# A two-layer graph network on one core: edge lags kept through the heads, last output products moved to the second period, layer 1's row splits and inverse degrees moved behind its keys and values

## The chip, the core and the metric

The kernel runs on one core of a Trainium2 chip. A core has five engines that run at the same time, each with its own list of instructions: the PE (TensorE, matrix products, with a separate record PEld for its weight loads), DVE (VectorE), ACT (ScalarE), POOL (GpSimd) and SP (SyncE, which here only issues transfers). They meet at semaphores. Transfers between the large memory (HBM) and the on-chip memory (SBUF) run on 16 DMA engines; they are issued from the queues of SP, ACT and POOL, and an instruction that issues a transfer can stand in its queue until what it needs is there. Products are summed up in a small memory of their own, PSUM.

The metric is the device time of one execution in microseconds (us), the median of several runs.

## What is computed

625 nodes with 1024 features, 10,000 edges. Two layers; each adds a graph part and an attention part that read the same normalized rows, and then a feed-forward part:

```python
edge_index = jnp.stack([src, dst])
xn = _layernorm(x)
x = x + _L0_gnn_ref(xn, edge_index, ...) + _L0_mix_ref(xn[None], ...)[0]
x = x + _L0_ffn_ref(_layernorm(x)[None], ...)[0]
xn = _layernorm(x)
x = x + _L1_gnn_ref(xn, src, dst, ...) + _L1_mix_ref(xn[None], ...)[0]
x = x + _L1_ffn_ref(_layernorm(x)[None], ...)[0]
```

The parts that the change touches:

```python
# layer 0, graph: attention over edges (4 heads of 64), with a loop at each node
e = jnp.einsum('ehd,hd->eh', leaky_relu(xl[src] + xr[dst], 0.2), att)
out = segment_sum(softmax_over_dst(e)[..., None] * xl[src], dst).reshape(n, 256) @ W_up
# both layers, attention without softmax (16 heads of 64, phi = elu + 1)
kv, ksum = einsum('nd,ne->de', phi(k), v), phi(k).sum(0)
out = (phi(q) @ kv) / (phi(q) @ ksum + eps) @ W_o + b_o
# layer 0, feed-forward with three-valued weights
silu(gate(x)) * up(x) -> down
# layer 1, graph: mean over incoming edges, twice
h = relu(x @ W_self0 + (sum_in(x) / max(deg, 1)) @ W_neigh0 + b0)
out = h @ W_self1 + (sum_in(h) / max(deg, 1)) @ W_neigh1 + b1
```

Layer 1's feed-forward part (attention, then eight experts of which each row uses two, and a shared one) is not touched by the change.

## The kernel before

The 625 rows stand in five blocks of 125 (NT = 5, index t); the 1024 features in eight blocks of 128 (KC = 8, index k or m); weights of 1024 columns are loaded in halves of 512 (class Half, index c), two transfers of 1 MB for each half, through a ring of buffers (wpool). The order on each engine is written out by hand. The helper `do` (class Stream) takes a piece of PE work and the vector work that follows it, and issues the vector work of one piece behind the PE work of a later one.

**Start (lines 361 to 570).** Rows are loaded, normalized and turned; edge numbers (si, di), att, the projection weights, the biases and the attention's weights are loaded. On SP's queue stand the rows, small weights, then the filling of `table` with zeros (625 x 625 pairs of nodes, padded, by 4 heads: 6.3 MB in HBM), and then, from `lin.half(0)`, the biases bk_t and bv_t and the weights Wk and Wv of layer 0's first half. The edge numbers and att are the first on ACT's queue. `left_right` makes xl and xr, which are written to HBM (xl_d, xr_d); `self_loops` makes the scores of the nodes' own loops, which are written to the table's diagonal (table<-own).

**Edges beside layer 0's attention (lines 575 to 790).** The 79 edge columns (128 edges each, the last 16) are worked in groups of two. For each column POOL issues a gather of xl rows (ga), a gather of xr rows (gb) and a scatter of the scores into the table, all indirect DMAs. A scatter waits for the landing of the one before. DVE adds, scales and reduces a group (lines 600, 572, 573), ACT takes the exponential (line 579). The function `work(us)` advances a planned clock by the PE work just issued, and issues the next group ("beat") when the clock passes its due time: 5.2 us a group at first, 8.5 from the seventh on. `lags` says how many groups score, exponential and scatter stand behind the gathers of the same beat; the value is cut by one for the last two of the eight heads (m >= 6), and set to 1, 1, 2 after them. What is left when the PE work is all issued follows in a loop without pacing.

Meanwhile the PE makes keys and values of both halves, then for every pair of heads m the query pq (line 130 through `query`), pd and po (`answer`; DVE then adds, takes the reciprocal, line 338, and multiplies: oT, line 339), and then the output products px with Wo, by `mixed(t)`: sixteen products for each block t. The sums of t = 3 and t = 4 are moved out of PSUM by DVE with the bias added (`kept`), since PSUM holds only three blocks (t = 0, 1, 2). Behind each block's px one of the three weight matrices of the feed-forward part is made three-valued by DVE (`ternary`).

**Feed-forward of layer 0, in periods p = 0 to 6 (lines 1011 to 1075).** The table is read back in five blocks (`load_table(t)`, tile tb, on POOL's queue), multiplied with the edge counts (`weigh`, tile pT, line 821), and multiplied with xl on the PE (`sums`, pg; then go, turned to goT, and `up_again`, px on top of the output products). Period p has sums of block p, and for block p - 1 the feed-forward: normalized rows, turned (ptr), gate and up (pgu), turned (phT), down (pdn), normalized again and turned (xnT1). The rows x are loaded again on POOL's queue, between the first block of the table and the second. From period 2 keys and values of layer 1 are put between (`spacer`); their weights are loaded by `lin1.weights(0)` in period 1.

**Layer 1 (lines 1077 to 1215).** Second half's keys and values, degrees (`degrees`), heads again by `query` and `answer`, and then the products of the mean (pa). For these the normalized rows are needed as two numbers, high and low (`rows_of`, `split`: DVE line 1144, ACT line 1117, DVE line 1119), ten pieces (two halves c, five blocks t). They and the inverse degrees (`inverses`) stand between the heads: two pieces after each of m = 0 to 3, one after m = 4 and 5, then the inverses. The biases b1 and bo are added to x on POOL (line 1161) after the heads.

Of the kernel before, what the change touches and what calls it, by code (L numbers as in the profile page):

```python
# [53 lines left out]
def attempt(ctx: ExitStack, tc: tile.TileContext, w: dict, out: bass.AP, shifted: bool):  # L54
# [161 lines left out]
    class LinearAttention:  # L216
# [17 lines left out]
        def half(self, c, loaded=False):  # L234
            Wk, bk, Wv, bv = (w[n] for n in self.names[1:])
            self.bk, self.bv = self.bias(bk, c, "bk_t"), self.bias(bv, c, "bv_t")
            if not loaded:
                self.weights(c)
            self.kf = mid([P, NT, 512], "kf")
            self.v = mid([P, NT, 4, 129], "v")  # L240
            nc.gpsimd.memset(self.v[:, :, :, 128:129], 1.0)
            self.kv.append(mix.tile([128, 4, 256], FP, tag="kv", name="kv", bufs=2))
# [101 lines left out]
    with ExitStack() as st0:  # L344
# [8 lines left out]
        with ExitStack() as edges:  # L353
# [10 lines left out]
            for dst, name in ((si, "src"), (di, "dst")):  # L364
                flat = w[name].rearrange("a b -> (a b)")
                nc.scalar.dma_start(out=dst[:, 0:EF], in_=flat[0:128 * EF].rearrange("(p t) -> p t", t=EF))
                nc.scalar.dma_start(out=dst[0:ER, EF:EN], in_=flat[128 * EF:E].rearrange("(p t) -> p t", t=1))
# [5 lines left out]
            for t in range(2, NT):  # L373
# [5 lines left out]
            nc.scalar.dma_start(out=att, in_=w["att"].to_broadcast([128, 256]))  # L379
# [5 lines left out]
            nc.gpsimd.memset(none, FAR if shifted else 0.0)  # L385
            nc.sync.dma_start(out=table.rearrange("(p a b) h -> p a (b h)", p=128, a=28),
                              in_=none.unsqueeze(1).to_broadcast([128, 28, 440]))
            sf = pool.tile([128, EN], FP, name="sf")
# [5 lines left out]
            def edge_numbers():  # L394
                for dst, src in ((sf, si), (df, di)):
                    nc.vector.memset(dst[:, EF:EN], -1.0)
                    nc.vector.tensor_copy(dst[:, 0:EF], src[:, 0:EF])
                    nc.vector.tensor_copy(dst[0:ER, EF:EN], src[0:ER, EF:EN])


                nc.vector.tensor_scalar(up, df, float(HN), None, op0=ALU.is_ge)
                nc.vector.scalar_tensor_tensor(dm, up, -float(HN), df, op0=ALU.mult, op1=ALU.add)
                nc.vector.tensor_scalar(up, up, 4095.0, 1.0, op0=ALU.mult, op1=ALU.add)

                row, col = (df, sf) if shifted else (sf, df)
                nc.vector.scalar_tensor_tensor(at, row, float(N), col, op0=ALU.mult, op1=ALU.add)
# [3 lines left out]
            if not shifted:  # L410
                nc.vector.tensor_scalar(att, att, 0.8, None, op0=ALU.mult)
# [128 lines left out]
            turn_x(1)  # L540
            root(0)
            for t in range(NT):
# [9 lines left out]
                if t == NT - 2:  # L552
# [4 lines left out]
            lin = LinearAttention(xnT, ("L0_Wq", "L0_Wk", "L0_bk", "L0_Wv", "L0_bv"), w["L0_bq"],  # L557
                                  lambda us: work(us), nc.sync)
            lin.half(0)
# [121 lines left out]
            def work(us):  # L681
                beat["us"] += us

                while beat["us"] >= 2.0 + 5.2 * min(beat["g"], 6) + 8.5 * max(beat["g"] - 6, 0) and chunks:
                    one_beat()
# [32 lines left out]
            def mixed(t, ks=range(KC), keep=None, then=None):  # L718
                for c in range(2):
                    def pe(c=c):  # L720
                        if c == 0 and ks[0] == 0:
                            hold["px", t] = ps2("px1")
                        for k in ks:
                            nc.tensor.matmul(hold["px", t][:P, c, :], lhsT=oT[:, k, nodes(t)], rhs=wo[c](k),  # L724
                                             start=(k == 0), stop=(k == KC - 1 and keep is not None))

                    def after():
                        px = hold.pop(("px", t))
                        for c in range(2):
                            nc.vector.tensor_tensor(keep[:, c, :], px[:P, c, :], bo[c][:P], op=ALU.add)  # L730

                    do(None, pe, after if keep is not None and c == 1 else None)
                    if then is not None and c == 0:
                        then()
                    work(0.87 * len(ks))
# [29 lines left out]
            for m in range(KC):  # L765
                if m >= KC - 2:
                    lags[:] = [n - 1 for n in lags]
                if m + 1 < KC:
                    lin.query(m + 1)
                else:  # L770
                    mixed(0, range(6))
# [15 lines left out]
            kept = mid([P, 2, 2, 512], "kept")  # L787
            mixed(3, keep=kept[:, 0], then=weight_sums)
            mixed(4, keep=kept[:, 1])
            weight_means()  # L790
            mixed(0, range(6, KC))
# [84 lines left out]
        def up_again(t):  # L876
            kept_apart = t >= 3
# [137 lines left out]
        load_table(1)  # L1015
# [9 lines left out]
        for p in range(NT + 2):  # L1025
# [6 lines left out]
            if p == 1:  # L1032
                lin1.weights(0)
# [23 lines left out]
            for t in ((0, 1), (2, 3, 4))[p] if p < 2 else ():  # L1057
                for c in range(2):
                    xc = x[:, t, c * 512:(c + 1) * 512]
                    nc.vector.tensor_tensor(xc, xc, bo[c][:P] if t < 3 else kept[:, t - 3, c, :], op=ALU.add)  # L1060
            if p == 1:
                lin1.half(0, loaded=True)
# [45 lines left out]
    def inverses():  # L1108
        nc.vector.reciprocal(dinv, dinv)
        own = mix.tile([P, NP], FP, tag="qe", name="own", bufs=1)[:, 0:N].rearrange("p (t n) -> p t n", t=NT)  # L1110
        nc.vector.tensor_tensor(own, dinv[:P, 0:N].rearrange("p (t n) -> p t n", t=NT),
                                ident[:P, :P].unsqueeze(1).to_broadcast([P, NT, P]), op=ALU.mult)
        nc.vector.tensor_reduce(dinvT, own, AX.X, ALU.add)
# [15 lines left out]
    degrees()  # L1129
    for t in range(1, NT):  # L1130
        lin1.key(t)
        lin1.value(t)
# [4 lines left out]

    xnh = [[midp.tile([P, NT, 512], NUM, tag="mid", name="xnh") for i in range(2)]]
    xnh.append([midp.tile([P, NT, 512], NUM, tag="mid", name="xnh"), sage.tile([P, NT, 512], NUM, name="xnl")])
    rows_left = [(c, t) for c in range(2) for t in range(NT)]  # L1140

    def rows_of(c, t):
        xh = mix.tile([P, 512], FP, tag=("kb", "ke")[t % 2], name="xh", bufs=1)
        nc.vector.tensor_scalar(xh, x[:, t, c * 512:(c + 1) * 512], mv1[:, t, 0:1],
                                rs1[:, t:t + 1], op0=ALU.subtract, op1=ALU.mult)
        split(xh, xnh[c][0][:, t, :], xnh[c][1][:, t, :])

    for m in range(KC - 1):
        lin1.query(m + 1)
        lin1.answer(m, oT)  # L1150
        for _ in range(2 if m < 4 else 1):
            if rows_left:
                rows_of(*rows_left.pop(0))
        if m == 5:
            inverses()
    assert not rows_left
    for name in ("b1", "L1_bo"):
        b_t = mix.tile([128, D], FP, tag="kv", name="b_t", bufs=2)
        nc.gpsimd.dma_start(out=b_t, in_=w[name].to_broadcast([128, D]))
        for t in range(NT):  # L1160
            nc.gpsimd.tensor_tensor(x[:, t, :], x[:, t, :], b_t[:P], op=ALU.add)
# [23 lines left out]
    for m in range(KC):  # L1185
        if m % 4 == 0:
            ws, wn = Half(wpool, w["W_self0"], m // 4), Half(wpool, w["W_neigh0"], m // 4)
            hT.append(mid([128, 4, NP], "hT"))
        a = m % 4
# [745 lines left out]
```

## Time and profile before

| | |
|---|---|
| median of 3 runs | 2213.21 us (2208.89 to 2214.76) |
| profiled execution | 2212.67 us |
| its span, first to last instruction | 2210.6 us |
| mean granted clock of the PE | 0.978 of full |
| transfers | 301.62 MB, 136 GB/s on the mean |
| POOL's scatters, page's row: table<-es,at | x79, 83.9 us, 1062 ns each |
| POOL's gathers: ga<-xl_d,si and gb<-xr_d,di | x79 each, 1041 and 998 ns |

The span is the time between the first and the last instruction in the record; the rest of the time of that execution lies outside of it. A row of a group has the line, engine and operation, the tiles written and read, the count, the busy time and the mean of one in ns, and then the idle time just before these instructions with what ended it. "PE pg L130 <- DVE pT L821" in a list of waits means: the PE stood before the product pg, issued at line 130, until DVE had written pT at line 821. The record of a product with float32 operands is two records of the PE. The row PEclk is the clock that the PE was granted, in tenths; at half clock a product takes twice as long, and this time counts as busy.

### The profile page before, as it was taken

What the parts mean: (1) busy time and instruction counts of PE and PEld (TensorE: products, weight loads), DVE (VectorE), ACT (ScalarE), POOL (GpSimd) and SP (SyncE); (2) the same over time, 40 slices, a digit from 0 to 9 for tenths busy, and PEclk for the clock granted to TensorE, in tenths of its full rate; (3) what the DMA queues carried; (4) which work ended last, traced back from release to release, by engine and by line L of the source; (5) the groups of instructions that cost most, each with busy time, mean ns of one, the idle gap of its engine ahead of it and who ended that gap; (6) DMA issues with size and microseconds to landing.
All of it is one profiled execution on the core that took longest, in us unless ns stands there. A gap on an engine that the chain in (4) does not pass through costs nothing. (4 is left out here: it accounts for less than half of the span.)

```text
span 2210.6 us, 17366 instructions
## 1 busy us (share of the span) xinstructions
PE 2119.9 (96%) x6934; PEld 1215.4 (55%) x6934; DVE 714.3 (32%) x1216; ACT 194.3 (9%) x354; POOL 342.3 (15%) x351
## 2 busy tenths in 40 slices
PE   7999997869899989999999999999999999999998
PEld 5665573445455667754446767457744444444443
DVE  4786486467421760000122133322011111111012
ACT  2010110002211200000000111100000000000000
POOL 1666776400000120010000000110000000000011
PEclk9999999869999999999999999999999999999999
DMA  9335432620122110240213111122099988997742
GB/s 293 92 98 180 146 113 79 161 66 22 44 80 76 48 48 1 76 161 20 76 38 105 38 39 38 29 95 94 8 361 345 331 306 295 330 330 285 275 143 92
DMA packets 145849, 301.62 MB, mean 136 GB/s; under 512 B 12371, under 2 KB 22437, under 8 KB 145755
## 3 DMA queue, kind: packets, MB, share of 16 engines
q1 hardware_dynamic: 123412, 243.18, 31.0%
q0 software_dynamic: 17664, 47.47, 7.1%
q10 hardware_dynamic: 4678, 9.72, 1.4%
q8 instruction: 58, 0.95, 0.2%
q14 instruction: 37, 0.30, 0.0%
HBM read 277.49 MB, written 22.84 MB: 136 GB/s over the span
## 5 line engine op out<-in xcount | busy, mean ns | idle before, releaser
L130 PE MATMUL pu<-w,xgT 128*128 128x512 f32 x768 | 333.9, 593 | 1.9 <-DVE xgT L1229 1.9
L130 PEld LDWEIGHTS pu<-w,xgT 128*128 128x128 f32 x768 | 144.0, 190 | 174.8 <-issue 171.9
L130 PE MATMUL pyb<-w,hb 128*128 128x512 f32 x384 | 174.3, 598 | 2.5 <-ACT yb L105 2.1
L130 PE MATMUL pk<-w,xnT 128*125 128x512 f32 x320 | 143.9, 603 | 3.8 <-DMA w<-in_L_Wk_dram 3.2
L130 PE MATMUL pv<-w,xnT 128*125 128x512 f32 x320 | 141.2, 594 | 0.0
L130 PE MATMUL pq<-xnT,w 128*128 128x313 f32 x512 | 138.1, 428 | 2.0 <-ACT qf L320 1.2
L130 PE MATMUL p<-tT,w 128*128 128x313 f32 x512 | 136.3, 428 | 0.4 <-DVE tT L1229 0.4
L130 PEld LDWEIGHTS pyb<-w,hb 128*128 128x128 f32 x384 | 69.8, 189 | 90.9 <-issue 74.8
L130 PEld LDWEIGHTS pq<-xnT,w 128*128 128x128 f32 x512 | 96.5, 190 | 42.1 <-ACT qf L320 3.7
L1769 DVE TENSOR_TENSOR su<-pu,su 128x512 f32<-128x512 f32 x24 | 16.6, 692 | 314.6 <-ACT su L1768 314.6
L130 PEld LDWEIGHTS p<-tT,w 128*128 128x128 f32 x512 | 96.8, 190 | 37.9 <-issue 1.2
L130 PEld LDWEIGHTS pk<-w,xnT 128*125 128x125 f32 x320 | 60.3, 191 | 77.8 <-issue 76.0
L130 PEld LDWEIGHTS pv<-w,xnT 128*125 128x125 f32 x320 | 60.0, 189 | 72.4 <-issue 71.8
L610 POOL DMA_INDIRECT table<-es,at x79 | 83.9, 1062 | 63.2 <-issue 33.7
L1752 POOL DMA_INDIRECT xg<-rows_d,slots x12 | 11.4, 947 | 524.7 <-PE pxg L1759 449.0
L592 POOL DMA_INDIRECT ga<-xl_d,si x79 | 82.3, 1041 | 29.6 <-issue 19.8
L592 POOL DMA_INDIRECT gb<-xr_d,di x79 | 78.9, 998 | 24.1 <-issue 23.5
L724 PE MATMUL px<-w,oT 128*125 128x512 f32 x160 | 71.1, 605 | 11.3 <-DVE z L337 11.3
L1119 DVE TENSOR_TENSOR z<-pz,z 125x512 fp32r<-125x512 f32 x10 | 6.9, 692 | 196.8 <-ACT z L1117 196.8
L130 PE MATMUL px<-w,hT 128*125 128x512 f32 x160 | 70.3, 592 | 0.0
L130 PE MATMUL px<-w,oT 128*125 128x512 f32 x160 | 70.3, 592 | 0.0
L130 PE MATMUL ph<-meanT,w 128*128 128x313 f32 x256 | 70.0, 426 | 0.0
(368 smaller groups left out, 2538.9 us busy)
## 6 DMA issues: line engine op xcount, KB each, us to landing
w<-in_eW_dram SPq DMA_DIRECT2D x144, 1024.0 KB
w<-in_L_Wk_dram SPq DMA_DIRECT2D x8, 1024.0 KB
w<-in_L_Wv_dram SPq DMA_DIRECT2D x8, 1024.0 KB
w<-in_L_Wq_dram SPq DMA_DIRECT2D x8, 1024.0 KB
w<-in_L_Wo_dram SPq DMA_DIRECT2D x8, 1024.0 KB
w<-in_W_self_dram SPq DMA_DIRECT2D x8, 1024.0 KB
w<-in_W_neigh_dram SPq DMA_DIRECT2D x8, 1024.0 KB
w<-in_sW_dram SPq DMA_DIRECT2D x8, 1024.0 KB
```

The lines of the kernel that those rows point to most:

```text
L130: nc.tensor.matmul(dst, lhsT=lhsT, rhs=rhs, start=(i == 0), stop=(i == len(pairs) - 1))
L592: nc.gpsimd.indirect_dma_start(out=ab[g][side][0:p, j, :], out_offset=None, in_=src[:, :], in_offset=bass.IndirectOffsetOnAxis(ap=ix[0:p, ...
L610: nc.gpsimd.indirect_dma_start(out=table[:, :], out_offset=bass.IndirectOffsetOnAxis(ap=at[0:p, lo + j:lo + j + 1], axis=0), in_=es[0:p, l ...
L724: nc.tensor.matmul(hold["px", t][:P, c, :], lhsT=oT[:, k, nodes(t)], rhs=wo[c](k), start=(k == 0), stop=(k == KC - 1 and keep is not None))
L1119: nc.vector.tensor_tensor(low, src, high.bitcast(FP), op=ALU.subtract)
L1752: nc.gpsimd.indirect_dma_start(out=xg, out_offset=None, in_=rows_d[:, :], in_offset=bass.IndirectOffsetOnAxis(ap=slots[:, b:b + 1], axis=0))
L1769: nc.vector.tensor_tensor(su, pu[:, 0, :], su, op=ALU.mult)
```

## The change

- **Start.** The loads of the edge numbers and of att move on ACT's queue behind `turn_x(1)`; att's scaling moves into `edge_numbers`. Biases and Wk of layer 0's first half are issued on SP's queue ahead of the zeros of the table, Wv behind them.
- **Edges.** A group from the seventh on is due every 8.1 us instead of 8.5. Lags are no longer cut in the last two heads, and the first output products, which stand in the last head, no longer advance the plan's clock.
- **Last output products.** `mixed(4)` moves from in front of the first period into period 1 (the second one), its halves at two places; its result stays in PSUM, and the bias is added as for t < 3. Layer 1's loads of Wk and Wv come behind it.
- **Table.** The second block of the table is loaded behind the first block of x instead of behind all five.
- **Layer 1.** The inverse degrees, in two pieces, and the five row splits of the first half go behind keys and values of t = 1 to 4. The heads m = 0 to 4 keep one row split each. The additions of b1 and bo on POOL move behind the heads and the mean products, to the stage of hT (m = 0 and m = 4), and their loads go to SP's queue.

```diff
@@ start @@
-            for dst, name in ((si, "src"), (di, "dst")):
-                ...
-            nc.scalar.dma_start(out=att, in_=w["att"].to_broadcast([128, 256]))
+            def load_edges():
+                for dst, name in ((si, "src"), (di, "dst")):
+                    ...
+                nc.scalar.dma_start(out=att, in_=w["att"].to_broadcast([128, 256]))
+            lin = LinearAttention(xnT, ("L0_Wq", "L0_Wk", "L0_bk", "L0_Wv", "L0_bv"), w["L0_bq"],
+                                  lambda us: work(us), nc.sync)
+            lin.biases(0)
+            lin.wk = Half(wpool, w["L0_Wk"], 0)
             nc.sync.dma_start(out=table.rearrange("(p a b) h -> p a (b h)", p=128, a=28),
                               in_=none.unsqueeze(1).to_broadcast([128, 28, 440]))
+            lin.wv = Half(wpool, w["L0_Wv"], 0)
             turn_x(1)
+            load_edges()
             root(0)
-            lin.half(0)
+            lin.half(0, loaded=True, biased=True)
@@ edges @@
-                while beat["us"] >= 2.0 + 5.2 * min(beat["g"], 6) + 8.5 * max(beat["g"] - 6, 0) and chunks:
+                while beat["us"] >= 2.0 + 5.2 * min(beat["g"], 6) + 8.1 * max(beat["g"] - 6, 0) and chunks:
-            def mixed(t, ks=range(KC), keep=None, then=None):
-                for c in range(2):
+            def mixed(t, ks=range(KC), keep=None, then=None, paced=True, cs=(0, 1)):
+                for c in cs:
-                    work(0.87 * len(ks))
+                    if paced:
+                        work(0.87 * len(ks))
-                if m >= KC - 2:
-                    lags[:] = [n - 1 for n in lags]
-                    mixed(0, range(6))
+                    mixed(0, range(6), paced=False)
-            kept = mid([P, 2, 2, 512], "kept")
-            mixed(3, keep=kept[:, 0], then=weight_sums)
-            mixed(4, keep=kept[:, 1])
+            kept = mid([P, 2, 512], "kept")
+            mixed(3, keep=kept, then=weight_sums)
+            mixed(0, range(6, KC))
             weight_means()
-            mixed(0, range(6, KC))
@@ periods @@
-            kept_apart = t >= 3
+            kept_apart = t == 3
             rows_dma(nc.gpsimd, x[:, t, :], xrows[t])
-        load_table(1)
+            if t == 0:
+                load_table(1)
             if p == 1:
-                lin1.weights(0)
+                mixed(4, cs=(0,))
-                    nc.vector.tensor_tensor(xc, xc, bo[c][:P] if t < 3 else kept[:, t - 3, c, :], op=ALU.add)
+                    nc.vector.tensor_tensor(xc, xc, kept[:, c, :] if t == 3 else bo[c][:P], op=ALU.add)
             if p == 1:
+                mixed(4, cs=(1,))
+                lin1.weights(0)
                 lin1.half(0, loaded=True)
@@ layer 1 @@
+    meanwhile = inverses() + [lambda t=t: rows_of(0, t) for t in range(NT)]
     for t in range(1, NT):
-        lin1.key(t)
-        lin1.value(t)
+        for f in (lin1.key, lin1.value):
+            f(t)
+            if meanwhile:
+                meanwhile.pop(0)()
     for m in range(KC - 1):
         lin1.query(m + 1)
         lin1.answer(m, oT)
-        for _ in range(2 if m < 4 else 1):
-            if rows_left:
-                rows_of(*rows_left.pop(0))
-        if m == 5:
-            inverses()
-    for name in ("b1", "L1_bo"):
-        ...
+        if m < NT:
+            rows_of(1, m)
         if m % 4 == 0:
             ws, wn = Half(wpool, w["W_self0"], m // 4), Half(wpool, w["W_neigh0"], m // 4)
             hT.append(mid([128, 4, NP], "hT"))
+            b_t = mix.tile([128, D], FP, tag="kv", name="b_t", bufs=2)
+            nc.sync.dma_start(out=b_t, in_=w[("b1", "L1_bo")[m // 4]].to_broadcast([128, D]))
+            for t in range(NT):
+                nc.gpsimd.tensor_tensor(x[:, t, :], x[:, t, :], b_t[:P], op=ALU.add)
```

In `rows_of`, the pieces of the first half write their normalized rows to the buffers of qf; those of the second half use kb and ke as before. `inverses` returns its two pieces instead of issuing them.

## The prediction

> **What bounds the kernel now.** I read the busy shares first, then the waits of the PE (TensorE), then the windows by stage, then the time order of the places where the PE waits. The page says:
>
> ```profile
> span 2210.6 us, 17366 instructions
> PE 2119.9 (96%) x6934; PEld 1215.4 (55%) x6934; DVE 714.3 (32%) x1216; ACT 194.3 (9%) x354; POOL 342.3 (15%) x351
> PEclk9999999869999999999999999999999999999999
> ```
>
> The PE is busy for 2119.9 of 2210.6 us, and the change removes no matrix product. So it can win only PE idle time and time in which the PE runs at half clock, which counts as busy. The windows by stage show where both are (columns: window, length, busy time and instructions of PE, PEld, DVE, ACT, POOL, granted clock, DMA share, GB/s):
>
> ```profile
> 0.00:48.00 48.00, 34.62 (x220) 28.56 (x220) 26.62 (x82) 12.52 (x26) 7.67 (x19) 1.00 0.90 277
> 48.00:409.00 361.00, 347.87 (x1255) 209.31 (x1256) 243.23 (x446) 35.51 (x95) 244.40 (x237) 0.98 0.36 117
> 409.00:448.00 39.00, 26.88 (x74) 15.70 (x72) 6.43 (x9) 1.66 (x2) 11.28 (x19) 0.73 1.00 255
> 448.00:630.00 182.00, 158.38 (x573) 92.99 (x574) 111.27 (x225) 34.30 (x56) 6.24 (x11) 0.88 0.19 58
> 630.00:707.00 77.00, 77.00 (x230) 39.92 (x229) 12.69 (x20) 7.22 (x13) 0.00 (x0) 1.00 0.16 55
> 707.00:812.00 105.00, 93.35 (x365) 66.55 (x364) 77.13 (x62) 16.77 (x25) 26.24 (x14) 0.95 0.15 51
> 812.00:2210.00 1398.00, 1381.85 (x4225) 762.38 (x4224) 236.94 (x373) 86.28 (x138) 46.45 (x51) 1.00 0.43 155
> ```
>
> Behind 812 us the PE is 98.8% busy at full clock. The losses are before: clock 0.73 and 0.88 around the hand-over from layer 0's edges to its feed-forward part (409 to 630), and 11.65 us idle in layer 1's heads (707 to 812). The waits of the PE name the causes (total, times, longest):
>
> ```profile
> PE pg L130 <- DVE pT L821: 12.0, 10, 6.4
> PE px L724 <- DVE z L337: 11.3, 1, 11.3
> PE po L130 <- DVE oT L339: 6.4, 7, 2.6
> PE pd L130 <- DVE z L337: 4.0, 1, 4.0
> PE pk L130 <- DMA w<-in_L_Wk_dram: 3.2, 1, 3.2
> ```
>
> The first is behind the edge chain. In time order, POOL's last scatter into the table, the load of the first block of that table, and the next loads:
>
> ```profile
> 409.18 0.85 POOL L610 DMA_INDIRECT table<-es,at  x1 [2.75 <-issue]
> 414.73 0.89 POOL L164 DMA_DIRECT2D tb<-table  x1 [4.70 <-DMA table<-es,at]
> 415.62 3.80 SPq L121 DMA_DIRECT2D w<-in_L_Wv_dram  x2
> ```
>
> The load lands at 424.27, and pg(0), the first product that needs it, starts at 425.39. From 53.47 to 409.18 POOL issues 237 indirect DMAs (79 groups of two gathers and a scatter, page rows of 1041, 998 and 1062 ns, with 0.30 between: 79 x 4.0 = 316 us of 356). So until pg(0) **POOL's edge chain sets the time**, not the PE.
>
> **The change, part by part** (all against this execution: 2212.67 us, 2210.6 of span and 2.07 around it; the median of the runs is 0.5 higher, which is nothing here).
>
> *A. Start.* Wk's load now goes on SP's queue ahead of the 6.3 MB of zeros (issued at 15.47, landed at 40.29), where bk_t waited until 40.31 and Wk landed at 48.07. pk then starts when the last left-right products end, about 45.6 instead of 48.69, and without a pause it keeps full clock: its sixteen records take 7.03 (the row of pv at 62.65) instead of 10.12. On the PE that is -6.2. Wv lies behind the zeros, which land about 6 us later (two 1 MB loads ahead at some 290 GB/s): Wv at about 52, needed at 57; covered. Edge numbers and att move behind turn_x(1) on ACT's queue: five issues of about 0.45 = 2.3 us in front of root(0), against a start that is free about 2.4 earlier. Both bounds for the first gather: -1 and +1; I take 0. If the zeros hold xl_d's last write on ACT's queue (they land at 46.5, it was issued at 46.27), it costs up to 1.
>
> POOL gets part of the 6.2: four scatters stood at 91.85, 101.14, 111.69 and 121.49 (3.17 + 1.13 + 2.64 + 1.21 = 8.15 us above the 0.30) for the write of own diagonal entries, which DVE makes between the PE's key and value pieces. Those come 6 us sooner: **-7** (-5 to -8).
>
> *B. The heads and the tail.* Lags are no longer cut for the last two heads, and the pace goes from 8.5 to 8.1. Before, DVE was standing in front of gathers, so z(7) was late: that is the 11.29 in front of px at 358.43. It goes; the PE reaches the end of its work before pg(0) earlier, and then waits for POOL, so of itself it is worth nothing. What is late next is the scatters. When the last gather was issued (gb at 391.17), 6 scatters were left, and they took until 409.18; in after 10 are left. Alone, scatters went every 2.4 to 5.1 us, since each waits for the landing of the one before and the ternary operations on DVE slow POOL (1.38, 1.85, 2.32 us instead of 1.0). From the gather at 344.57 to the last landing (414.0) before took 69.4. After: 24 (remaining gathers with their scatters) + 11 + 3 + ten scatters at 2.7 to 3.0 + 2.2 to 4.8 = 67 to 73. I take **0**, with -2 and +4 as ends.
>
> The load of the first block took 9.5 us with layer 1's 4 MB of Wk and Wv beside it (408.75 to 419.05). In after these loads wait for the last output products. Later blocks took 7.5 (459.32 to 466.8) and 7.2 (495.51 to 502.7): **-2**. Here the Trainium skill's page "DMA: Bandwidth & Descriptors", section "Queues, rings and completion order", speaks: an engine serves its queues in turn, by packets. With two queues of equal right, the 1.22 MB would take up to twice 7.3, so +7 instead of the measured +2. I keep the rows, since the load overlaps only a part of the weights. Against it: the second block now follows x(0), not x(4), on the same queue; behind the first, so free.
>
> pg(0) starts 7 + 0 + 2 = **9 earlier**, at about X = 416.4.
>
> *C. Second period.* The second output product (mixed(4), 16 x 2 records of 0.43: 14.0 us of PE) moves from in front of pg(0) into period 1. There the PE had waits: 3.59 (448.34), 2.07, 4.12, 2.47 and 4.24 (483.86). The rule that speaks against this is the page "TensorE: Matmul & The Clock Gate", section "HAM oscillation": idle stretches of over about 3.4 us halve the clock. In the trace 8 px took
>
> ```profile
> 470.34 5.72 PE L884 MATMUL px<-wu,goT 128*125 128x512 f32 x8
> 506.82 3.60 PE L884 MATMUL px<-wu,goT 128*125 128x512 f32 x8
> ```
>
> in this period and in the next. Since POOL's chain still ends last, the PE, 14 us of work the poorer, now idles some 20 us before pg(0), where it idled 6.37: cold in both. By the rule, with waits of 3.6 and more left in, mixed(4) stays at half clock and costs 28. By the trace the half clock granted from 423.4 on ended at 443.9, inside the first px, and came back at 447.3 behind the 3.59 wait; mixed(4)'s first half now fills that wait, so I take 14. My walk from X: c0 of mixed(4) waits for px(0)'s PSUM (X+20.6) and ends at X+27.7; pg(1) 4.6 at full clock (448.34 to 459: over 8) ends at X+32.3, where before it ended at X+35. gu's products end at X+36.2 (before X+40.2); c1 runs X+36.8 to 43.8 while DVE makes room; px(1) at full clock to X+47.8; down-products X+51.1 (X+53.15); pg(2) X+59.1 (486.55 = X+61.2). Load_table(1) right behind x(0) makes this possible: weigh(1) can follow go(0) at X+11.7 instead of waiting for a block that landed at 446.8 (X+21.4). So 14 us of products go in and the period ends 2 (cold to its end) to 6 (warm) earlier: **-3**. The two additions for t=4 stay two; key and value loads are needed only at X+71 and land by X+60.
>
> *D. Layer 1.* Here is the surest part. In its heads DVE and not the PE sets the pace:
>
> ```profile
> 776.44 8.69 PE L130 MATMUL pq<-xnT,w 128*128 128x313 f32 x32 [0.25 <-ACT qf L320]
> 789.17 2.46 PE L130 MATMUL pd<-qf,kv 128*128 128x313 f32 x4 [4.04 <-DVE z L337]
> 794.18 2.45 PE L130 MATMUL po<-qf,kv 128*128 128x313 f32 x4 [2.56 <-DVE oT L339]
> ```
>
> A head is 8.43 + 1.06 + 1.05 = 10.54 us on the PE. The loop through DVE and ACT is oT to qe 0.78, qf 0.68, the product 0.81, two row splits of 1.85 (0.54 + 0.63 + 0.69), z 0.84, reciprocal 4.07, oT 0.81: 11.85 (the heads from 729.13 to 740.98 take just that). With one row split it is 10.0, so the PE bounds. The inverses (4.05 + 2.68 + 0.81), after m = 5, made the 4.04, and with it 2.46 for a pd of 1.06 (half clock). All of this goes behind the second half's keys and values, where DVE is idle 4 to 6 us of every 7 and three PSUM buffers lie between; 3 + 5 insertions of 1 to 4 us are hidden there. If they were not, 7.5 + 5 x 1.85 = 17 would come back in full. From pq at 707.07: seven heads at 10.54 give 780.9, then pa, pd and po of the last head 787.4, where it was 804.05: **-16.6** (-13 to -17.5). POOL's additions (10 x 2.35) and their loads, which also stood beside DVE here (2.28 for a 0.69 subtraction), go to the first product stage of layer 1, where the PE is bound and x is next read at 1010.0 (line 1278); on SP the b_t load stands between weight loads and its wait is for a free buffer: 0, at worst 1.
>
> **Sum:** -9 - 3 - 16.6 = -28.6, so 2212.67 - 28.6 = 2184. I say 2185, as none of the ends of B is a gain.
>
> **Rivals.** (1) *Own writes do not help, and ten scatters take longer than six:* the tail runs at 3.5 us each, and POOL's 7 is eaten. For it: the scatters before already averaged 3. Against it: ternary work is over sooner. Then -2 - 3 - 13 to -16 gives 2193 to 2197. Chance 0.25. (2) *The second period runs at full clock and the tail is short:* -13 - 6 - 17.5: 2176. For it: load_table(1) and 14 us of dense work. Against it: DVE waits of over 3.4 us remain. Chance 0.15. (3) *Slower:* mixed(4) is exposed. The PE stays at half clock from pg(0) through the period, so 14 us cost 28 and fill waits of only 7; with POOL's chain 3 later (+3), +24 outweighs 16.6: 2220. It decides once the sum of waits filled is under 11 and the clock is half throughout. Against it: the rows at 442 to 447. Chance 0.05. (4) *Row splits not hidden behind keys and values:* 2185 + 8 = 2193 to 2200, chance 0.05. My forecast 0.50.
>
> **Numbers.** 2185. Below it rival 2, above it rivals 1 and 4: low 2173, high 2199 leave out the slow side and the extreme of rival 2. A measurement of this kernel tells 0.3% (6.6 us) from no change; only the slower rival and the worst of rival 1 lie there: faster 0.92, same 0.03, slower 0.05.
>
> **What would show it.** pk before 47 and sixteen records in 7.0; no wait of over 2 us for own entries near 92; last scatter near 402; pg(0) near 416; no wait for z in front of px; pg(2) 59 to 60 behind pg(0); every head of layer 1 in 10.5. It is wrong if the last scatter comes at 409 again, or mixed(4)'s records take 0.85 each.

## The result, and the profile after

The changed kernel takes 2197.91 us (median of 5 runs, 2196.15 to 2202.00), the kernel before 2214.76 beside it: a ratio of 0.9932, 95% interval 0.9919 to 0.9945. By this ratio it is 15 us less (the two medians differ by 16.9), where 28 were forecast. Two more sets of runs of the changed kernel gave 0.9936 (0.9918 to 0.9954) and 0.9951 (0.9934 to 0.9968), so 11 to 15 us is the gain. The profiled execution has a span of 2195.8 us, 14.8 less than before. Its page and its list of the PE's waits:

```profile
span 2195.8 us, 17365 instructions
PE 2109.7 (96%) x6934; PEld 1210.8 (55%) x6934; DVE 712.2 (32%) x1214; ACT 194.1 (9%) x354; POOL 340.7 (16%) x349
PEclk9999999689999999999999999999999999999999
```

```profile
PE pg L130 <- DVE pT L828: 24.2, 5, 23.2
PE po L130 <- DVE oT L342: 4.8, 2, 2.5
PE px L733 <- DVE kept L739: 4.7, 1, 4.7
PE pk L130 <- DMA w<-in_L_Wk_dram: 1.6, 1, 1.6
```

The wait of px for z (11.3) and that of pd for z (4.0) are gone, as forecast. The wait of pg for pT has grown from 6.4 to 23.2 in one piece: the PE has less to do before the first period and stands for POOL's chain, which ends hardly earlier. And two waits of po for oT are left in layer 1, where none was forecast:

```profile
766.73 2.04 PE L130 MATMUL po<-qf,kv 128*128 128x313 f32 x4 [2.46 <-DVE oT L342]
786.54 1.39 PE L130 MATMUL po<-qf,kv 128*128 128x313 f32 x4 [2.30 <-DVE oT L342]
```

Where the 14.8 us come from is read by cutting both spans at the same instructions (starts in us, from the order in time):

| stretch | before | after | difference | forecast |
|---|---|---|---|---|
| start to pg(0) | 425.39 | 419.66 | -5.7 | -9 |
| pg(0) to pg(2) | 61.2 | 56.9 | -4.3 | -3 |
| pg(2) to pq(1) of layer 1 | 220.5 | 225.4 | +4.9 | 0 |
| pq(1) of layer 1 to hT's first product | 117.5 | 107.6 | -9.9 | -16.6 |
| from there to the end | 1386.1 | 1386.3 | +0.2 | 0 |

One execution has luck in it, so the same cuts were made in all traces of programs that are the same in a stretch. The last two rows repeat within 0.5 us, the second within 1.6. The first does not: with the start and edges of before, pg(0) came at 425.39 and 422.65, on the mean 424.0; in the unchanged repetitions of the changed kernel at 419.66, 424.83 and 422.08, on the mean 422.2. So the -5.7 of this pair stands for some -2, which the spread does not tell from nothing. Of the third row's +4.9, 2.0 lie between pg(2) and pg(4) and come with the change; the other 2.9 are a matter of the PE's clock (both below).

### The profile page after: what moved, and what is told of

The parts are those of the page before. It is cut to its first block, busy times and chain, and to the rows that moved or that the text cites. A ratio compares the mean times of both kernels' runs of the same rounds, so it can differ in the third digit from the quotient of the medians.

```text
span 2195.8 us, 17365 instructions
## 1 busy us (share of the span) xinstructions
PE 2109.7 (96%) x6934; PEld 1210.8 (55%) x6934; DVE 712.2 (32%) x1214; ACT 194.1 (9%) x354; POOL 340.7 (16%) x349
## 5 line engine op out<-in xcount | busy, mean ns | idle before, releaser
L1783 DVE TENSOR_TENSOR su<-pu,su 128x512 f32<-128x512 f32 x24 | 16.6, 692 | 314.6 <-ACT su L1782 314.6
```

The source lines that it names most:

```text
L1783: nc.vector.tensor_tensor(su, pu[:, 0, :], su, op=ALU.mult)
```

## The experiments

Ten edited kernels answer the questions that the table leaves; three of them were run in two sets of runs, and the changed kernel was run twice more. In one set (own_early, second_back, last_head and no_start) the edge chain was some 50 us longer: the kernel before took 2262.88 there. Why is not known. The record gives its chip the same number as in the two sets after it, where the kernel before took 2211.68 and 2213.33. Issuing its 237 transfers took POOL as long as elsewhere (245 us in own_early and in the changed kernel), but its gathers stood for DVE's scores (44.8 us in own_early; the changed kernel has no such wait), and behind pg(0) all stretches were as elsewhere. Ratios are to the kernel before in the same set; the changed kernel was not run in that one.

**Layer 1 alone, start alone.** The kernel before with the hunks of one part of the diff.

```diff
 # l1_only: before, and
+    meanwhile = inverses() + [lambda t=t: rows_of(0, t) for t in range(NT)]
...
 # start_only: before, and
+            lin.wk = Half(wpool, w["L0_Wk"], 0)
...
+            lin.wv = Half(wpool, w["L0_Wv"], 0)
...
+            load_edges()
```

> The kernel before with the layer 1 part of the change alone. My reading of the changed kernel's trace: this part gave 11.4 us up to the last head's po and lost 1.6 behind it, since POOL adds b1 to x at 748 to 760, beside DVE's work of the sixth head (a row split took 2.57 and 2.29 us instead of 0.54 and 0.69), and po then stood 2.46 us. Theory: about 2203 against 2213 (-9 to -12), with the slow row split again. Rival (the prediction's own figure): -16.6, 2196; then the loss in the changed kernel comes from an earlier part.

> The kernel before with the start part alone. Theory: the last write of xl_d stands on ACT's queue until the zeros of the table have landed, so the first gather starts near 56.3 instead of 53.5; the scatters' waits for the nodes' own entries go (8 us), so the last scatter lands 4 to 5 us earlier than 414.0 and the time is 4 to 5 us shorter (about 2208). Rival: the first gather's delay goes right through, no scatter gains, the time is 0 to 3 us longer.

Layer 1 alone: 2204.16 us, ratio 0.9962 (0.9950 to 0.9974), so -8.4; its stretch from pq(1) to hT took 107.57, with a wait of po for oT of 2.65. The stretch and the wait are those of the theory, the time is just short of its -9 to -12, and -16.6 is ruled out; more than half of the whole gain is here. The start alone: 2213.11 us, ratio 0.9995 (0.9985 to 1.0006), no change that can be told. The first gather started at 56.97, as expected, but the last scatter landed at 410.5 and pg(0) started at 422.7, which is where layer 1 alone, with the old start, also had it (422.65). That is nearer the rival, but the first gather's delay did not come through either.

**Why the first gather is late.** In the changed kernel, the issues of xl_d's last block on ACT's queue and the first gather on POOL's:

```profile
46.71 0.38 ACTq L164 DMA_DIRECT2D xl_d<-xlr  x1
51.10 0.31 ACTq L165 DMA_DIRECT2D xl_d<-xlr  x1
51.44 1.28 ACT L258 ACT_TABLE_LOAD   x1 [4.77 <-DMA table<-none]
```

```profile
56.34 1.17 POOL L601 DMA_INDIRECT ga<-xl_d,si  x1 [8.19 <-issue]
```

The second piece of the write stood from 47.1 to 51.1; what it waited for is named by the next line of ACT, the zeros of the table. In the kernel before it was issued at 46.62 and the first gather at 53.47. Why a write of xl_d must wait for the zeros is not shown. So this block goes to POOL's queue:

```diff
-                    rows_dma(nc.scalar, xl_d.rearrange("(t p) e -> t p e", p=P)[t], xlr[:, t, 0:256])
+                    rows_dma(nc.scalar if t < NT - 1 else nc.gpsimd, xl_d.rearrange("(t p) e -> t p e", p=P)[t], xlr[:, t, 0:256])
```

> The changed kernel, but the last block of xl_d is written from POOL's queue and not from ACT's. Theory: the write no longer stands behind the zeros of the table, the first gather starts at 54 to 55 instead of 56.3, the last scatter lands 1.5 to 2.5 us earlier, the time is 1.5 to 2.5 shorter (about 2195.5). Rival: the chain has slack further on (waits for landings at 165 to 195), so that the last scatter lands at 409 to 410 again and the time doesn't change.

2194.59 us, ratio 0.9919 (0.9900 to 0.9937). The first gather came at 53.09, so the cause of its lateness is shown:

```profile
53.09 1.04 POOL L601 DMA_INDIRECT ga<-xl_d,si  x1 [4.19 <-DMA xr_d<-xlr]
```

But the last scatter was issued at 407.54, against 407.81: the rival is right for the chain, whose length is not set by its start alone. The time's interval overlaps that of the changed kernel; no gain is shown.

**Why the scatters wait near 100.** In the changed kernel, POOL's transfers and the write of own entries around 97:

```profile
94.64 0.99 POOL L619 DMA_INDIRECT table<-es,at  x1 [0.30 <-issue]
95.93 0.96 POOL L601 DMA_INDIRECT ga<-xl_d,si  x1 [0.30 <-DVE gs L581]
96.84 0.31 ACTq L164 DMA_DIRECT2D table<-own  x1
97.19 0.41 ACTq L165 DMA_DIRECT2D table<-own  x1
97.19 0.95 POOL L601 DMA_INDIRECT gb<-xr_d,di  x1 [0.30 <-issue]
99.78 0.99 POOL L619 DMA_INDIRECT table<-es,at  x1 [1.64 <-DMA table<-own]
```

Both write the same table, and each waits for the other. The scatter of 94.64 landed at 96.77; the own write was issued 0.07 later; it landed near 98.9, and the next scatter went at 99.78. The same pairs stand at 105.86 and 105.92, and at 115.10 and 115.17. In the prediction these waits came from late keys and values. They are a turn between two queues, and an earlier PE does not shorten them: with the old start (layer 1 alone) they came to 4.1 us, with the new one (start alone) to 4.2. The test puts all five writes ahead of the first scatter:

```diff
-                if 5 <= g < NT + 5:
-                    self_loops(g - 5)
+                if 1 <= g < NT + 1:
+                    self_loops(g - 1)
```

> The changed kernel, with the scores of the nodes' own loops made and written four groups earlier, so that all five writes to the table's diagonal come ahead of the first scatter. My reading: from the third on, such a write waits for the scatter before it and the next scatter for the write (own write issued at 96.84, the scatter before landed at 96.77, own landed 98.88, next scatter 99.78), 1.3 us three times, whatever the PE and DVE do. Theory: these waits go (4.1 us of extra waiting between the 25th and 48th of POOL's transfers becomes under 1), the last scatter comes 2 to 4 us earlier counted from the first gather, the time is 2 to 4 shorter than the changed kernel's. Rival (the prediction's): the waits come from late keys and values, so they stay.

> The changed kernel with the five own-loop writes ahead of the first scatter, this time beside the changed kernel on one chip. Theory: the three waits of 1.3 us near 100 to 120 are gone, last scatter minus first gather 2 to 4 us shorter than in the changed kernel beside it, time 2 to 4 shorter. Rival: the chain gives the gain back at the weight loads near 165 to 185, where scatters wait 9 to 10 us, so nothing is left at the last scatter.

In the set with the longer chain it took 2256.44 us, ratio 0.9963 (0.9945 to 0.9981). In the other: 2194.18, ratio 0.9927 (0.9907 to 0.9947), beside 0.9936 for the changed kernel. The trace of this second run has, at the same place:

```profile
91.58 1.31 POOL L619 DMA_INDIRECT table<-es,at  x1 [0.30 <-issue]
93.20 0.97 POOL L601 DMA_INDIRECT ga<-xl_d,si  x1 [0.31 <-issue]
94.47 0.95 POOL L601 DMA_INDIRECT gb<-xr_d,di  x1 [0.30 <-issue]
95.72 0.99 POOL L619 DMA_INDIRECT table<-es,at  x1 [0.30 <-issue]
```

The waits above the usual 0.30 between POOL's 25th and 48th transfer, 4.1, 5.7 and 4.1 us in the three traces of the changed kernel, are 0.1 here. (With the longer chain other waits fall there too: 6.2 with this edit, 12.9 to 18.5 in the three other traces of that set.) From first gather to last scatter it took 349.6 us, against 351.5, 355.7 and 353.0 in the three traces of the changed kernel: 2 to 6 us less. The mechanism is shown; the time of this edit alone is not told from noise.

**Start undone in the changed kernel.**

```diff
-            load_edges()
             root(0)
...
-            lin.half(0, loaded=True, biased=True)
+            lin.half(0)
```

> The changed kernel with the start as it was before. Theory: the start part gains nothing (the first gather is 1 to 3 us later with it, the PE's gain is waited off in front of pg(0)): 2196 to 2199, first gather at 53.5 to 55.5, last scatter landed at 408 to 412. Rival (the prediction's -7 for the own entries): 2202 to 2205.

> The changed kernel with the start as before, beside the changed kernel. Theory: the start part gains nothing, within 3 us of the changed kernel, first gather 1 to 4 us sooner, three waits for own entries of 1.1 to 3 us, last scatter at 405 to 413 in both. Rival (the prediction): 5 to 8 us longer than the changed kernel.

> The changed kernel once more, for a second trace and as the mark for the three beside it. If the clock's answer to the PE's waits of 2.70 and 2.95 us (in the periods after pg(4)) is a matter of the execution, the stretch from pg(2) to layer 1's second query takes 220.5 to 222.3 where no or one half-clock window falls there and 223.5 to 225.5 where two do; the other stretches come out as before within 0.5 us (pg(0) to pg(2) 56.9, query to hT 107.6).

> The changed kernel, as the mark for the two beside it: pg(0) to pg(2) 56.9 to 58, first gather 56 to 58, 2196 to 2200 where before takes 2211 to 2214.

In the set with the longer chain the ratio was 0.9994 (0.9979 to 1.0009). In the other: 2200.60 us, ratio 0.9942 (0.9926 to 0.9957), and the changed kernel beside it 2200.99, ratio 0.9951. So no gain of the start part is seen either way; start alone, whose interval ends at -3.3 us, rules the -7 out. That the first gather would come sooner without it was a miss: it came at 57.44. With the old start it came at 53.47, 55.49, 55.53 and 57.44, with the new one at 56.3 to 57.8 in most traces and once at 55.62; what moves it in the old one is not known.

**Lags cut again, moved products put back.**

```diff
 # lags_cut: the changed kernel, and
             for m in range(KC):
+                if m >= KC - 2:
+                    lags[:] = [n - 1 for n in lags]
 # second_back: the changed kernel, and
+            mixed(4, keep=kept[:, 1])
...
-            if t == 0:
-                load_table(1)
+        load_table(1)
...
-                mixed(4, cs=(0,))
+                lin1.weights(0)
```

> The changed kernel with the lags cut in the last two heads as before the change, the only part of the edge change that is undone. Theory: the PE stands 8 to 11 us in front of px for z of the last head again, but that is covered by the 23 us that it stands in front of pg(0); six instead of ten scatters are left after the last gather (22 instead of 31.4 us), while the last gather comes 6 to 9 us later: last scatter 0 to 4 us earlier, time 0 to 4 us shorter. Rival (the change's reason): the late z comes through to pg(0), 5 to 10 us longer.

> The changed kernel with mixed(4) in front of the first period again, the second block of the table behind all of x and layer 1's loads where they were: start, edges and layer 1 as changed. Theory (this part gave most of what the first 500 us gained): block 0 of the table takes 9.5 instead of about 8 us to load, pg(0) to pg(2) takes 61 to 62.4 instead of 56.9; the time is 5 to 7 us longer than the changed kernel's, 2203 to 2205. Rival (the edge chain gave it): 0 to 3 us longer.

> The changed kernel with mixed(4) in front of the first period, the second block of the table behind all of x and layer 1's loads where they were, beside the changed kernel. Theory: from the last scatter to pg(0) 14 to 16 us instead of 12, pg(0) to pg(2) 61 to 62.5 instead of 57 to 58, the time 5 to 9 us longer. Rival: 0 to 3 us longer.

Lags cut: 2200.08 us, ratio 0.9946 (0.9928 to 0.9964), the changed kernel beside it 0.9936. The list of the PE's waits:

```profile
PE pg L130 <- DVE pT L830: 19.8, 5, 18.8
PE po L130 <- DVE oT L342: 8.1, 4, 2.6
PE pd L130 <- DVE z L340: 5.0, 1, 5.0
```

In layer 0 the PE again stands for z (5.0, in front of pd) and, behind it, for oT (2.6), and the wait in front of pg(0) is shorter for it; the last scatter came at 412.66, against 413.29. The late z is covered, as expected; eight scatters instead of ten were left after the last gather, and no time was won. The pace of 8.1 us was not tested alone.

Products put back: in the set with the longer chain 0.9997 (0.9977 to 1.0017), with pg(0) to pg(2) in 62.5 against 56.9 to 58.1 in its neighbours. But in the other set 2202.74, ratio 0.9956 (0.9940 to 0.9972), beside 0.9951: no difference that can be told. My theory is not confirmed there, and the trace suggests why. The windows from pg(0) to pg(2) of the kernel before, the changed kernel, and this one (columns as before):

```profile
425.39:486.55 61.16, 40.39 (x130) 28.00 (x130) 37.83 (x67) 6.38 (x11) 7.64 (x13) 0.61 0.53 130
```

```profile
419.66:476.54 56.88, 43.87 (x163) 27.18 (x163) 37.85 (x67) 6.39 (x11) 6.97 (x13) 0.80 0.65 183
```

```profile
427.31:482.76 55.45, 35.82 (x131) 24.12 (x131) 37.93 (x67) 6.39 (x11) 7.30 (x13) 0.65 0.43 110
```

The 14 us of products that the second has and the third has not make 1.4 us of difference here (3.0 at most, in the changed kernel's other traces). Where before lost its time is in front of pg(1): it came 22.95 us behind pg(0), and 17.96 in the third, which is 5.0 of the 5.7 us between the two. There before waited for the second block of the table:

```profile
447.16 4.83 DVE L821 TENSOR_TENSOR pT<-tb,CT 125x500 f32<-125x500 f32 x5 [10.14 <-DMA tb<-table]
448.34 0.65 PE L130 MATMUL pg<-xl,pT 125*125 125x65 f32 x2 [3.59 <-DVE pT L821]
```

Layer 1's first weights were issued then from 408.75 on and the last of them landed about 444; the second block of the table landed at 447.07. With the products put back but the lags kept, the PE is through its heads sooner:

```profile
401.15 3.81 SPq L121 DMA_DIRECT2D w<-in_L_Wk_dram  x2
408.01 3.80 SPq L121 DMA_DIRECT2D w<-in_L_Wv_dram  x2
```

These landed by 416.5, ahead of the table's first block (425.4), and the second block landed at 442.0. In the set with the longer chain the same kernel's weights came together with the table, and there the stretch took 62.5:

```profile
467.57 0.38 SPq L121 DMA_DIRECT2D w<-in_L_Wk_dram  x1
468.08 0.90 POOL L164 DMA_DIRECT2D tb<-table  x1 [2.52 <-PE px L733]
```

So lags kept (weights early, when the heads end early enough) and products moved (weights late) each can take the same collision away, which is why taking out one of them showed nothing in the time. With both out, as in layer 1 alone and start alone, the stretch took 62.3 and 62.4. This is argued from traces that agree; no run moved the loads alone.

Part of the gain is given back. From pg(2) to pg(4) it took 61.1 to 61.4 us in the five traces with mixed(4) in front of pg(0), and 61.7 to 63.2 in the twelve with it in the second period. Why was not looked for.

**Heads of layer 1.** In the changed kernel, DVE's work with the last row split, beside POOL's additions, and SP's load for them:

```profile
754.25 1.21 DVE L324 SCALAR_TENSOR_TENSOR qf<-qe,qf 128x626 f32<-128x626 f32 x1 [2.15 <-ACT qf L323]
755.39 2.57 DVE L1151 TENSOR_SCALAR xh<-x,mv,rs 125x512 f32<-125x512 f32 x1
758.66 2.29 DVE L1132 TENSOR_TENSOR xnl<-xh,xnh 125x512 fp32r<-125x512 f32 x1 [0.69 <-ACT xnh L1130]
```

```profile
744.28 0.34 SPq L1200 DMA_DIRECT2D b_t<-in_b_dram  x1
```

```profile
747.81 9.86 POOL L1202 TENSOR_TENSOR x<-x,b_t 125x1024 f32<-125x1024 f32 x4 [135.62 <-DMA b_t<-in_b_dram]
758.04 2.35 POOL L1202 TENSOR_TENSOR x<-x,b_t 125x1024 f32<-125x1024 f32 x1 [0.36 <-DVE xh L1151]
```

The additions stand in the text behind the mean products, but on POOL's queue nothing is in front of them and their load has a free buffer once head 3 is through. So they ran here, and not in hT's stage as the prediction said. The Trainium skill, page "SBUF — State Buffer", section "SBUF: two separate sides", says that DVE and GpSimd share a pair of ports as an exclusive lock, held for a whole instruction. It names the DVE operations that take part: those in a mode with two ports, and those with two inputs in SBUF beside a GpSimd operation that reads SBUF. The rows agree: the two operations took 2.57 and 2.29 us, where they take 0.54 and 0.69 without additions beside them (rows below), and they ended at 757.96 and 760.95, just behind the additions that ended at 757.67 and 760.39. The second has two such inputs; whether the first is in a mode with two ports, no run shows. Both additions are put behind the second stage's weights on SP's queue:

```diff
+            for name in ("b1", "L1_bo") if m == 4 else ():
-            b_t = mix.tile([128, D], FP, tag="kv", name="b_t", bufs=2)
-            nc.sync.dma_start(out=b_t, in_=w[("b1", "L1_bo")[m // 4]].to_broadcast([128, D]))
+                b_t = mix.tile([128, D], FP, tag="kv", name="b_t", bufs=2)
+                nc.sync.dma_start(out=b_t, in_=w[name].to_broadcast([128, D]))
 # last_head: this, and
-        if k == 1:
+        if k == 2:
             lin1.answer(KC - 1, oT)
```

> The changed kernel, but both biases are added to x on POOL in the second stage of hT (m = 4), their loads behind that stage's weights on SP's queue, so that POOL has nothing to do beside the heads. Theory: all seven heads of layer 1 take 10.54 us, the wait of 2.46 for oT goes with its half clock, 4 to 5.5 us shorter than the changed kernel (about 2193). Rival: the row split is slow from another cause (the weight loads), then the same wait of 2 to 3 us stays and the time is as before it, 2197 to 2198.

> The changed kernel with the additions of both biases in hT's second stage, and the last head's answer behind the second mean product instead of the first. The wait of po for oT (2.30 us at 786.54) comes from DVE's chain of z, reciprocal and oT (5.8 us), against 3.3 us of one mean product and 1.1 of pd. Theory: with two products that wait goes and the heads end without a half clock: 2 to 4 us shorter than with the late additions alone (2193.5), so about 2190.5. Rival: the wait moves to the mean products, which need a PSUM buffer; no gain, 2193 to 2194.

Late additions: 2193.54 us, ratio 0.9906 (0.9888 to 0.9923). The additions now run in one piece at 877, no head of the seven waits, and the stretch from pq(1) to hT took 103.14 instead of 107.57:

```profile
756.33 0.54 DVE L1151 TENSOR_SCALAR xh<-x,mv,rs 125x512 f32<-125x512 f32 x1
757.56 0.69 DVE L1132 TENSOR_TENSOR xnl<-xh,xnh 125x512 fp32r<-125x512 f32 x1 [0.69 <-ACT xnh L1130]
764.39 1.22 PE L130 MATMUL pd<-qf,kv 128*128 128x313 f32 x4
765.45 1.22 PE L130 MATMUL po<-qf,kv 128*128 128x313 f32 x4
766.51 8.59 PE L130 MATMUL pq<-xnT,w 128*128 128x313 f32 x32
```

The last head's answer behind the second mean product: that stretch took 99.80, another 3.3 less, so DVE's z, reciprocal and oT were what po stood for. It ran in the set with the longer chain (2250.26 us, ratio 0.9941, interval 0.9921 to 0.9961), so its time is not to be set beside 2193.5.

**All of these together.** Late additions, last head, own writes early, and xl_d's last block on POOL.

> The changed kernel with late additions of the biases, the last head's answer behind the second mean product, the own-loop writes ahead of the first scatter, and the last block of xl_d written from POOL's queue. Sum of the parts: -4.4 (heads), -3.3 (last head), -2 to -4 (own), -0 to -2 (xl_d): 10 to 13 us shorter than the changed kernel beside it. Rival: only the 7.7 of layer 1 arrive, since the edge chain gives back what it is spared.

2182.49 us, ratio 0.9862 (0.9842 to 0.9882), beside 0.9936 for the changed kernel: 16 us better than it, where 10 to 13 were expected; the intervals (some 4 us each way) do not tell the two apart. It has both halves: pq(1) to hT in 99.79, first gather at 52.87 and last scatter at 401.51, while the PE stands 26.0 us in front of pg(0). From first gather to last scatter it took 348.6 us, and 349.6 with early own writes alone; in the other traces outside the set with the longer chain it took 351.5 to 357.5. So in these two traces the earlier first gather does come through to the last scatter. With xl_d's block on POOL alone it did not (354.5), and the parts were not taken apart further.

## Why the prediction was right or wrong

Some 13 us of the forecast gain did not come. Two terms of the sum account for about as much: POOL's 7 us in A, which did not exist, and in D nearly 8 us that POOL's additions and the last head's wait cost, which were put at nothing or left out.

**What bounds the kernel:** right. POOL's chain sets pg(0), the PE's gains ahead of it are waited off (23.2 us there), and behind hT nothing moved.

**A, start, "-7 (-5 to -8)":** this failed in whole. The PE's part came as worked out (pk at 45.10, sixteen records in 7.03). The step that failed is "POOL gets part of the 6.2": the scatters' 8.15 us were put down to late keys and values. In truth each own write waits for a scatter and each scatter for an own write, 4.1 us whatever the PE does; the other 4 us of that one trace were not there in the next trace of the same start (4.1 in layer 1 alone). "I take 0" for the first gather, with +1 as the bound, was short too: the zeros were expected to land at 46.5, and the write behind them went at 51.1 to 52.2, so that the first gather came at 56.3 to 57.6 in the changed kernel's traces, against 53.1 with that write on POOL's queue. The length of the chain stayed at 351.5 to 355.7 us, before and after alike.

**B, tail, "0, -2 to +4":** right. Ten scatters were left after the last gather, and from the last gather of xl (ga) to the last issue it took 31.4 us, against 20.1 to 22.3 in the traces of the old edges; that gather came 8 us earlier on the mean.

**The table's first block, "-2":** right in size. Between the last scatter and pg(0) there are 11.5 to 12.0 us in the changed kernel's traces and 14.1 to 16.2 in the three with the old order and lags, of which part is the scatter's own landing under the loads (4.8 us in the trace of before, 1.9 in that of after).

**C, second period, "-3":** the size was right (56.9, 57.8 and 58.4 us against 61.2, 62.3 and 62.4), less up to 2 us given back behind it. The reason was half right. That pg(1) would no longer wait for a late second block was the forecast and came true. But the forecast gave the lateness to the block's place behind x alone. By the traces some 7 us of it are the collision with layer 1's weights (the block landed 21.7 us behind pg(0) in before, 14.7 with the products put back), which the kept lags can take away too, and then the place of mixed(4) wins nothing (argued, not tested alone). "Before it ended at X+35" was misread: pg(1) of before ended at 459.03, 33.6 behind pg(0). The clock rule that I weighed against it speaks of idle stretches; mixed(4)'s first half took 7.13 us for sixteen records, at nearly full clock, so the row was the better guide.

**D, layer 1, "-16.6 (-13 to -17.5)":** the mechanism was right (heads at 10.54 us but for one, DVE no longer in the loop), the size -9.9. The failed terms are "0, at worst 1" for POOL's additions, which ran beside the heads and not in hT's stage and cost 4.4 (107.57 to 103.14), and the last head's wait, which the sum left out and which cost 3.3 (103.14 to 99.80). With both mended the stretch gained 117.5 - 99.8 = 17.7. (The terms of the old loop add up to 11.69, not 11.85; 11.85 is what the heads took, and nothing hangs on the difference.)

**What the prediction did not have:** the clock's luck in the stretch behind pg(2). The waits of 2.70 and 2.95 us (for room, in the periods after pg(4)) are the same in every trace, but the PE is at half clock after the first of them only in some. The same eight products behind the 2.70, changed kernel and late additions:

```profile
569.76 1.90 PE L948 MATMUL ptr<-ident,room 125*128 125x125 f32 x8 [2.70 <-DVE room L925]
```

```profile
573.99 1.04 PE L948 MATMUL ptr<-ident,room 125*128 125x125 f32 x8 [2.70 <-DVE room L925]
```

And the 40 us around both waits, in the same order:

```profile
552.00:592.00 40.00, 34.35 (x92) 16.94 (x91) 21.83 (x46) 8.79 (x13) 0.00 (x0) 0.87 0.16 53
```

```profile
556.00:596.00 40.00, 34.01 (x99) 16.46 (x98) 21.74 (x46) 8.79 (x13) 0.00 (x0) 0.96 0.15 53
```

Clock 0.87 in one and 0.96 in the other, with equal waits. From pg(4) to pq(1) of layer 1 it took 158.9 to 162.3 us over the traces, so some 3 us of one trace's difference can be luck, and 2.9 of it fell into this comparison. The first rival of the prediction, "own writes do not help", named the failed step of A and was the nearest in time. Its own terms give 2192 to 2195, not the 2193 to 2197 it states. And its other half, a tail at 3.5 us a scatter, did not come (31.4 us for ten), so that its time lay near was in part luck.

## What to carry to other kernels

An instruction moved down in the text moves in time only if something on its own queue or in its data holds it: ask what is in front of it there. When two queues write one tensor, find out which waits for which before crediting the wait to a third engine; a wait that stands at the same distance behind its partner each time is a turn, not lateness. And when two parts of a change can each remove one collision, taking out one at a time may show nothing, so look for the collision in the trace.

## What the runs showed of the hardware

The half clock came after waits well below what I had weighed. The wait of 2.70 us stands in all seventeen traces; within 2 us of it a half-clock stretch began in twelve, and in five (before, layer 1 alone, xl_d's block on POOL, late additions, and products put back outside the set with the longer chain) none did. The last head's wait of 2.3 us (po at 786.54) was followed by one in twelve traces of thirteen. The Trainium skill, page "TensorE: Matmul & The Clock Gate", section "HAM oscillation — how this bites in real kernels", puts the limit at gaps of about 3.4 us. Here the measurement decides: waits of 2.3 to 2.7 us can bring the half clock too, and what decides in one execution is not shown.
